# Attention scores on TensorE: seven bf16 parts in quarter columns, or two float32r parts in half rows

## The chip, the cores and the metric

One core of one Trainium2 chip runs the whole program in one launch. The metric is device time in microseconds, lower is better: the median of three runs of the kernel before is 895.65 us (894.32 to 899.57). The core has five engines that run side by side and wait for one another by semaphores: TensorE (PE in the profile; its weight loads are listed apart, as PEld), VectorE (DVE), ScalarE (ACT), GpSimd (POOL) and SyncE (SP, which here only issues DMA transfers).

## The reference, cut to what matters

The input is x of shape (2, 2048, 256) in float32. It is layer-normed to xn. Then the output is x plus a causal attention of xn plus a spectral feed-forward part of xn (a 256x256 matrix that the kernel works out once).

```
q = rope((xn @ wq).reshape(B, S, 16, 16)); k = rope((xn @ wk).reshape(B, S, 4, 16)); v = ... 4 heads
scores = einsum('bshd,bthd->bhst', q, k) / 4          # head_dim 16, 16 query heads on 4 key heads
attn   = softmax(where(causal, scores, -inf))
out    = x + einsum('bhst,bthd->bshd', attn, v).reshape(B, S, 256) @ wo + real(ifft(fft(xn) @ w)) + bias
```

The contraction of a score runs over only 16 dimensions, and it has to come out with nearly float32 exactness.

## The kernel before, in words

The 2 x 2048 rows are cut into 8 blocks of 512 rows: j = 0 to 3 along the sequence, b = 0 and 1 alternating. A block has four groups g of four query heads, so there are 32 units (n, g), eight for each j. Each unit works through its scores twice.

**First pass, row maxima (kind "A" in the planner).** `maxima` works out, for 128 rows and up to 512 keys, the scores with rows on the 128 partitions, and VectorE takes the maximum over the keys. Off the diagonal this is `row_max`: one PSUM tile `sm` holds two heads side by side (2 x 512 columns, two banks) and one TENSOR_REDUCE of 1024 elements reads it. On the diagonal, `first_rows` and `last_rows` build tiles `sd` whose 32-row pieces are laid out with turned order, so that masked parts are mostly left out: two tiles of 576 and four of 800 elements for a unit, reduced into `top_g`. `parts` puts the pieces together with two more reductions, splits the negated maxima into three bf16 parts with five further reductions, and `spread` turns them on TensorE (`ps_m`), copies them to `mt`, and sends `mt` by a DMA on ACT's queue into three rows of the unit's query tile `qst`.

**Second pass, probabilities (kind "B").** `scores` works out the same scores with keys on the partitions and 512 query rows as columns, the row maximum already subtracted by the three extra contraction rows (`kst` holds -1 there); ScalarE takes exp from PSUM (`st`, one bank for one head; `sp`, two banks, once all maxima are done) into `es`. For j > 0 GpSimd zeroes the masked triangles in `es`; for j = 0 TensorE adds a mask product. **Third, values (kind "V").** `values` multiplies `es` in float32 with `va` into `av` (four heads in four 32-column strips of TensorE), ScalarE copies `av` to `avs`, and a chain of DMAs, a reciprocal and a multiplication on GpSimd makes `attT`, from which `output` works out `po`, to which VectorE adds the residual `xr`.

**How a float32 score is made.** Rotated q and k (`raw`) are split on GpSimd (on VectorE for the first block) into three bf16 parts h, m, l by `split`: cast, subtract, cast, subtract. Seven products of parts are stacked along the contraction: `QPART = "hmlhmhm"` against `KPART = "hhhmmll"`, 7 x 16 = 112 rows, plus three for the maximum = 115 rows. The stacks `qst` and `kst` are filled by DMAs from SP (`stack`, `stack_runs`, the latter through a copy in HBM). Every product of the kernel except the transposes runs through `matmul` with 32 output partitions, four such instructions side by side in four column strips (`product`), which makes 128 partitions.

**What sets the order.** The kernel writes its own order, one instruction list per engine. A planner loop at the end keeps a clock for each engine, gives each piece a cost and the pieces it needs, and at each step picks among A, B, V, S (`spread`), F (late pieces) and M (other pieces). `due`, `AHEAD`, `RATE` and `WINDOW` say how far the maxima run ahead. The costs only shape the order; on the chip each engine takes its list in order and waits on semaphores. PSUM has eight banks: three of `st`, two double banks of `s` (`sm`, `sd`, later `sp`) and one of `av`.

Of the kernel before, what the change touches and what calls it, by code (L numbers as in the profile page):

```python
# [11 lines left out]
BF16 = mybir.dt.bfloat16  # L12
AF = mybir.ActivationFunctionType
# [4 lines left out]
P = 128  # L18
# [5 lines left out]
def tile_attn_plus_spectral_ffn(  # L24
# [47 lines left out]
    QPART = "hmlhmhm"  # L72
    KPART = "hhhmmll"
    KC = DH * len(QPART)
    KA = KC + 3
# [43 lines left out]
    def matmul(to, lhsT, rhs, **more):  # L119
        issued[0] += 2 if lhsT.dtype == BF16 else 4  # L120
        nc.tensor.matmul(to, lhsT, rhs, **more)  # L121
# [4 lines left out]

    def use(eng, us, needs=(), gives=()):
        clock[eng] = max(clock[eng], ready(needs)) + us
        if eng == "pe":
            at = issued[0] // LOADED  # L130
            for k in range(max(loaded), at + 1):
                clock["pe"] = max(clock["pe"], loaded[k])
                loaded[k + 1] = clock["pe"] + LOAD
            clock["pe"] = max(clock["pe"], loaded[at])
        for k in gives:
            there[k] = clock[eng] + LATE[eng]

# [47 lines left out]
    def load_x(n):  # L185
# [25 lines left out]
    ident_h = const.tile([P, P], BF16, name="ident_h")  # L211
    nc.vector.tensor_copy(ident_h, ident)

    mask = const.tile([P, P], BF16, name="mask")
    nc.gpsimd.memset(mask, 0.0)
    nc.gpsimd.affine_select(
        out=mask, in_=mask, pattern=[[-1, P]], compare_op=ALU.is_ge, fill=NEG, base=0,
        channel_multiplier=1,
    )

    mask_t = const.tile([P, P], BF16, name="mask_t")
    nc.gpsimd.memset(mask_t, 0.0)
    nc.gpsimd.affine_select(
        out=mask_t, in_=mask_t, pattern=[[1, P]], compare_op=ALU.is_ge, fill=NEG, base=0,
        channel_multiplier=-1,
    )
# [8 lines left out]

    turned_h = const.tile([P, P], BF16, name="turned_h")
    for q in range(0, P, QD):
        nc.vector.tensor_copy(turned_h[:, q : q + QD], ident_h[:, P - QD - q : P - q])

    G0, TE, TO, STEP = 10, 7, 35, 19
    top_g = const.tile([P, 2, NKV, 3 * STEP], F32, name="top_g")
    nc.vector.memset(top_g, NEG)
    nc.vector.memset(top_g[:, :, :, 0:3], 0.0)
    nc.vector.memset(top_g[:, :, :, 38:41], 0.0)
    rows_g = top_g.rearrange("p r h c -> p (r h) c")
    nc.gpsimd.affine_select(
        out=rows_g[:, :, 0:3], in_=rows_g[:, :, 0:3], pattern=[[0, 2 * NKV], [-QD, 3]],
        compare_op=ALU.is_ge, fill=NEG, base=-QD, channel_multiplier=1,  # L250
    )
    nc.gpsimd.affine_select(
        out=rows_g[:, :, 38:41], in_=rows_g[:, :, 38:41], pattern=[[0, 2 * NKV], [QD, 3]],
        compare_op=ALU.is_ge, fill=NEG, base=QD - 1, channel_multiplier=-1,
    )
# [157 lines left out]

    xnT, va, kst, qst = {}, {}, {}, {}

    def ones(n):
        e, eng, us = nc.gpsimd, "pool", 2.5 if n == 0 else 2.9
        va[n] = const.tile([P, NI, NKV, QD], F32, tag=f"va{n}", name=f"va{n}")
        e.memset(va[n], 1.0)
        kst[n] = const.tile([P, NKV, SB], BF16, tag=f"kst{n}", name=f"kst{n}")  # L420
        for h in range(NKV):
            e.memset(kst[n][96:P, h, :], -1.0)
        use(eng, us, (), [("ones", n)])

    def project(n):
# [99 lines left out]
        def stack(c, a_part, f):  # L525
            src = part[c][f * HP : (f + 1) * HP, "hml".index(a_part), :]
            for a in range(len(QPART)):
                if (KPART if c == NK else QPART)[a] == a_part:
                    to = kst[n] if c == NK else qst[n, 2 * c + f]
                    gives = []  # L530
                    if a == len(QPART) - 1 if c == NK else a_part == "l":
                        gives = [("kst", n) if c == NK else ("stk", n, 2 * c + f)]
                        gives += [("part", at[c, "part"])] * (c == NK)
                    needs = [("part", "in", n, c, a_part)]
                    later(to[a * DH : (a + 1) * DH, :, :], src, 64, needs, gives)

        def stack_runs(c, units):

            runs = {}
            for f in units:  # L540
                g = 2 * c + f
                runs[g] = dram.tile([3, HP, SB], BF16, tag="run", bufs=4, name=f"run{n}_{g}")
                later(
                    runs[g].rearrange("a r s -> r a s"), part[c][f * HP : (f + 1) * HP, :, :],
                    192, [("part", "in", n, c, "l")],
                    [("run", n, g)] + [("part", at[c, "part"])] * (f == 1),
                )
            for g, run in runs.items():
                rows = run.rearrange("a (d h) s -> (a d) (h s)", h=NKV)
                for lo, hi in ((0, 3), (3, 5), (5, 7)):  # L550
                    later(
                        qst[n, g][lo * DH : hi * DH, :, :], rows[0 : (hi - lo) * DH, :],
                        64 * (hi - lo), [("run", n, g)], [("stk", n, g)] * (hi == 7),
                    )
# [18 lines left out]
        def split(c, k):  # L573
            r = rows(c)
            if k == 0:
                if c < NK:
                    for g in (2 * c, 2 * c + 1):
                        qst[n, g] = work.tile(
                            [P, NKV, SB], BF16, tag="qst", bufs=8, name=f"qst{n}_{g}"
                        )  # L580
                        take_slot("qst")
                part[c] = work.tile([P, 3, SB], BF16, tag="part", bufs=3, name=f"part{n}_{c}")
# [5 lines left out]
            elif k == 1:  # L588
                ra[c] = work.tile([P, SB], F32, tag=f"ra{min(n, 1)}", bufs=1, name=f"rb{n}_{c}")
                e.tensor_tensor(ra[c][:r], raw[c][:r], part[c][:r, 0, :], ALU.subtract)  # L590
                use(eng, SUB, (), [("raw", at[c])])
            elif k == 2:
                e.tensor_copy(part[c][:r, 1, :], ra[c][:r])
                use(eng, CAST, (), [("part", "in", n, c, "m")])
                if direct(c, 0):
                    stack(c, "m", 0)
            else:
                e.tensor_tensor(part[c][:r, 2, :], ra[c][:r], part[c][:r, 1, :], ALU.subtract)
                use(eng, SUB, (), [("part", "in", n, c, "l")])
# [21 lines left out]
        for c in (NK, 0, 1):  # L621
# [6 lines left out]
                (eng, [], [], lambda c=c: split(c, 2)),  # L628
                (eng, [], [], lambda c=c: split(c, 3)),
# [6 lines left out]
    np_of, np_parts, made = [], [], []  # L636
    for a in range(2):
        of = const.tile([P, NI, 3, NKV, 2], F32, name=f"np_of{a}")
        nc.vector.memset(of, 0.0)
        np_of.append(of)  # L640
        np_parts.append(
            of.rearrange("p i a h b -> p (i a h b)").bitcast(BF16)
            .rearrange("p (i a h b) -> p i a h b", i=NI, a=3, h=NKV)[:, :, :, :, 3]
        )

    def maxima(n, g):
        b, j = blocks[n]
        t = {}
        slots, slots_done = [], []

        def begin():
            if not slots_done:
                t["mx"] = work.tile(
                    [P, 2, 2, NKV, NJ], F32, tag="mx", bufs=3, name=f"mx{n}_{g}"
                )
            slots_done.append(1)

        def pair_of(name):
            t["slot"] = take_slot("s")
            t["ps"] = ps_s.tile([P, 2, SB], F32, tag="s", name=name)  # L660

        def rows_of(h, i, q):

            at = i * P + (q if i % 2 == 0 else P - QD - q)
            return qst[n, g][0:KC, h, at : at + QD]

        def on_pe(k, us):
            use(
                "pe", us,
                [("stk", n, g), ("kst", at_block[b, k]), ("s", t["slot"] - ring["s"])],  # L670
                [("pair", t["slot"])],
            )

        def on_dve(cols, out, of):
            nc.vector.tensor_reduce(out, of, AX.X, ALU.max)  # L675
            use("dve", 0.07 + cols / 960, [("pair", t["slot"])], [("s", t["slot"])])

        def row_max(i, k, pr):


            def head(e):
                if e == 0:
                    begin()
                    pair_of(f"sm{n}_{g}_{i}_{k}_{pr}")
                h = 2 * pr + e
                on_pe(k, SB * 4.28e-4 + 0.003)
                for q in range(0, P, QD):
                    matmul(
                        t["ps"][q : q + QD, e, :], rows_of(h, i, q),
                        kst[at_block[b, k]][0:KC, h, :], start=True, stop=True,  # L690
                    )
                if e == 1:
                    r, odd = divmod(i, 2)
                    on_dve(2 * SB, t["mx"][:, odd, r, 2 * pr : 2 * pr + 2, k], t["ps"])

            needs = [("stk", n, g), ("kst", at_block[b, k])]
            return lambda: head(0), lambda: head(1), 2 * SB + 150, needs

# [3 lines left out]
        def keys(h, lo, hi):  # L702
            return kst[n][0:KC, h, lo:hi]

# [805 lines left out]
```

## Time and profile before

| what | value |
|---|---|
| median of three runs | 895.65 us (894.32 to 899.57) |
| the profiled execution, first to last instruction (its span; the profile gives no other time for it) | 892.9 us |
| what lies around the span, against the median | 2.75 us |
| granted TensorE clock | 1.000 |
| groups of scores for the maxima: `sm` matmuls, `sd` tiles | 3072 matmuls, 192 tiles |
| ScalarE exponentials | 1006 of one bank, 41 of two |
| transfers | 62.67 MB, mean 70 GB/s |

The page gives each engine's busy time over the span, and a chain of work that is followed back from the last instruction. A matmul's duration in the profile includes the time to fill and drain the array; matmuls of a stream overlap, so what one costs is read from the distance between starts, or from the chain, and not from its duration. A number of matmuls such as "x8" next to a time means eight 32-column instructions, that is two heads of 128 partitions.

### The profile page before, as it was taken

How to read it: one execution, taken by the hardware profiler on the slowest of the kernel's cores; microseconds unless marked ns; L12 is line 12 of the kernel's file. 1: busy time of each engine (PE TensorE's matmuls, PEld its weight loads, DVE VectorE, ACT ScalarE, POOL GpSimd, SP SyncE). 2: the span in 40 equal slices, each digit the busy share in tenths (PEclk: the TensorE clock that was granted, in tenths of full speed). 3: DMA queues.
4: the chain of work that ended last, by engine and by line, in shares of the span. 5: the costliest groups of instructions: out<-in, count | busy, mean ns of one | idle time of the engine just before them, and what ended most of it. 6: DMA issues, size and time to landing. Idle time of an engine off the chain costs nothing.

```text
span 892.9 us, 37137 instructions
## 1 busy us (share of the span) xinstructions
PE 877.8 (98%) x16596; PEld 475.6 (53%) x16596; DVE 728.6 (82%) x1002; ACT 637.1 (71%) x1188; POOL 364.1 (41%) x491
## 2 busy tenths in 40 slices
PE   8999999999999999999999999999999999999997
PEld 5666555555555555555544555565455555545443
DVE  7888887897969995999978899979889889798401
ACT  4276737687768875888747877858597887579885
POOL 8778757725933334631357121212652011101111
PEclk9999999999999999999999999999999999999999
DMA  5555733521451002430014300110241001100000
GB/s 180 133 148 135 203 96 96 160 71 39 111 148 62 27 29 83 106 106 14 20 50 120 97 28 14 39 51 14 60 115 60 14 3 40 50 14 15 27 2 25
DMA packets 42543, 62.67 MB, mean 70 GB/s; under 512 B 9080, under 2 KB 32360, under 8 KB 42384
## 3 DMA queue, kind: packets, MB, share of 16 engines
q1 hardware_dynamic: 32960, 41.83, 17.4%
q0 software_dynamic: 8128, 17.69, 6.2%
q8 instruction: 130, 2.13, 1.1%
q10 hardware_dynamic: 1296, 0.79, 0.3%
q14 instruction: 29, 0.24, 0.1%
HBM read 32.75 MB, written 18.40 MB: 57 GB/s over the span
## 4 chain that ended last, share of the span: by engine, by line
PE 90%; DVE 4%; ACT 3%; DMA 1%; issue 1%; ACTq 0%; SPq 0%; POOL 0%; DVEq 0%; POOLq 0%
PE av L121 25%; PE st L121 24%; PE sm L121 19%; PE sd L121 7%; PE po L121 6%; PE ps_q L121 4%; ACT es L946 2%; PE sp L121 2%; DVE top_g L675 2%; PE idle L125 1%; PE ps_x L125 1%; DMA qst<-run 1%; PE ps_ff L121 1%; PE ps_m L121 1%; DVE mx L675 1%
## 5 line engine op out<-in xcount | busy, mean ns | idle before, releaser
L946 ACT ACTIVATE es<-st 128x512 f32<-128x512 f32 x1006 | 533.1, 604 | 153.7 <-PE st L121 133.3
L675 DVE TENSOR_REDUCE mx<-sm 128x2 f32<-128x1024 f32 x384 | 450.0, 1216 | 39.2 <-PE sm L121 38.2
L121 PE MATMUL st<-qst,kst 115*32 115x512 bf16 (+9 forms) x4744 | 337.1, 345 | 0.2
L121 PE MATMUL av<-es,va 128*32 128x512 f32 (+3 forms) x2560 | 288.9, 529 | 1.3 <-ACT avs L1017 0.4
L121 PE MATMUL sm<-kst,qst 112*32 112x512 bf16 x3072 | 236.2, 379 | 0.7 <-DMA qst<-run 0.4
L121 PEld LDWEIGHTS <-kst 115*32 115x32 bf16 x5120 | 162.3, 95 | 136.0 <-issue 58.4
L121 PEld LDWEIGHTS <-qst 112*32 112x32 bf16 x5632 | 150.3, 96 | 128.0 <-issue 83.0
L675 DVE TENSOR_REDUCE top_g<-sd 128x25 f32<-128x800 f32 (+1 forms) x192 | 168.2, 906 | 35.3 <-PE sd L121 34.5
L964 POOL TENSOR_SCALAR_AFFINE_SELECT es<-es 128x512 f32<-128x512 f32 (+1 forms) x120 | 65.3, 546 | 236.1 <-ACT es L946 234.7
L121 PEld LDWEIGHTS av<-es,va 128*32 128x32 f32 x2560 | 82.2, 109 | 48.3 <-issue 18.3
L121 PE MATMUL sd<-kst,qst 112*32 112x384 bf16 (+11 forms) x2560 | 101.3, 256 | 2.3 <-DVE top_g L675 1.8
L1038 POOL DMA_DIRECT2D res<-avs x30 | 18.0, 601 | 105.7 <-ACT avs L1017 102.6
L121 PEld LDWEIGHTS <-ident_h 128*32 128x32 bf16 x1344 | 45.5, 96 | 27.0 <-issue 20.1
L1152 DVE TENSOR_TENSOR xr<-po,xr 128x256 f32<-128x256 f32 x36 | 15.2, 423 | 48.7 <-PE po L121 45.7
L121 PE MATMUL sd<-mask,ident_h 128*32 128x64 bf16 x1024 | 52.9, 193 | 0.1
L121 PE MATMUL ps_q<-xnT,wp 128*32 128x512 f32 x384 | 46.7, 594 | 0.2 <-ACT xnT L460 0.2
L946 ACT ACTIVATE es<-sp 128x1024 f32<-128x1024 f32 x41 | 39.7, 1027 | 6.1 <-PE sp L121 5.9
L475 ACT COPY raw<-ps_q 128x512 f32<-128x512 f32 x24 | 14.1, 587 | 34.9 <-PE ps_q L121 30.2
L560 POOL TENSOR_TENSOR ra<-raw,cs 128x512 f32<-128x512 f32 (+1 forms) x21 | 27.1, 1290 | 23.6 <-ACT raw L475 22.7
L121 PE MATMUL po<-wo_sb,attT 128*32 128x256 f32 x512 | 34.2, 380 | 0.0
L121 PE MATMUL po<-mff,xnT 128*32 128x256 f32 x512 | 33.7, 379 | 0.0
L1063 POOL DMA_DIRECT2D sums<-den x15 | 8.1, 540 | 61.7 <-DVE den L1057 61.7
(112 smaller groups left out, 614.2 us busy)
## 6 DMA issues: line engine op xcount, KB each, us to landing
qst<-run SPq DMA_DIRECT2D x62, 128.0 KB
res<-avs POOLq DMA_DIRECT2D x30, 256.0 KB, 2.9
run<-part SPq DMA_DIRECT2D x31, 192.0 KB
qst<-run SPq DMA_DIRECT2D x31, 192.0 KB
sw<-raw SPq DMA_DIRECT2D x70, 64.0 KB
xr<-in_L_attn_x_dram SPq DMA_DIRECT2D x16, 256.0 KB
attT<-res POOLq DMA_DIRECT2D x15, 256.0 KB, 4.2
inv<-sums POOLq DMA_DIRECT2D x15, 256.0 KB, 3.6
```

Of the source, the lines that this page charges most:

```text
L121: nc.tensor.matmul(to, lhsT, rhs, **more)
L125: nc.tensor.transpose(to, of, unit)
L475: nc.scalar.copy(raw[c], ps)
L560: e.tensor_tensor(ra[c][:r], raw[c][:r], cs[j][:r, 0, :], ALU.mult)
L675: nc.vector.tensor_reduce(out, of, AX.X, ALU.max)
L946: nc.scalar.activation(to, of, AF.Exp, scale=SCALE)
L964: nc.gpsimd.affine_select(out=to, in_=to, pattern=pattern, compare_op=ALU.is_ge, fill=0.0, base=0, channel_multiplier=-1,)
L1038: nc.gpsimd.dma_start(out=res[n, c][f], in_=avs[u])
L1063: nc.gpsimd.dma_start(out=sums, in_=den[n, c])
L1152: nc.vector.tensor_tensor(xr[n, r][:, e, :], po, xr[n, r][:, e, :], ALU.add)
```

## The change

* `split` makes two parts: h is `raw` rounded to float32r (a 4-byte type of TensorE), l is what is left, rounded. `QPART, KPART = "hlhl", "hhll"`: four products of 16 rows, the last cut by two dimensions, 62 rows, plus two for the maximum = 64 rows. Two of four GpSimd steps of `split` go.
* Heads of even number stand in rows 0 to 63 of `qst` and `kst`, heads of odd number in rows 64 to 127; a tile holds two heads along the columns. One score product is one instruction of 64 rows with 128 output partitions, and the one for the other half (the other head, another PSUM bank) follows it (`side_by_side`). Values, projections and outputs stay in 32-column strips.
* Diagonal row scores: five whole tiles of 1024 elements for a unit (`second_rows`, two of `first_rows`, two of `last_rows`). Masks are added by bf16 products with `eye` and `over` (`shut`), two for each half. The layout tricks with `top_g`, `turned_h` go.
* `parts` is one reduction, one copy and one subtraction (in place of seven reductions). `spread` is one product with a 32x128 result, `mt` has two parts, and its two small DMAs for a unit are issued by SP (stream `lasts`), not by ACT.
* `stack` and `stack_runs` issue more and larger DMAs: a query tile is filled by four of 128 KB in the planner's count, `run` holds two 4-byte parts.
* The planner keeps a clock for each half of the rows, books a cost for the change between halves and 32-column strips, starts the later blocks' preparation eight tiles earlier (`- 8`), and has new rules for the pick: it prefers to stay with A and B once it works in halves. In the order that comes out, TensorE changes between kinds of tiling 697 times.

The diff, cut to its core:

```
-    QPART = "hmlhmhm"
-    KPART = "hhhmmll"
-    KC = DH * len(QPART)
-    KA = KC + 3
+    KC = HP - 2
+    QPART, KPART = "hlhl", "hhll"
...
+    def use_half(half, us, needs, gives):
+        at = max(pe_start(half), ready(needs))
+        if not halves[0]:
+            half_free[:] = [at, at]
+        halves[0] = True
+        clock["pe"] = at
...
-        kst[n] = const.tile([P, NKV, SB], BF16, tag=f"kst{n}", name=f"kst{n}")
+        kst[n] = const.tile([P, 2, SB], F32R, tag=f"kst{n}", name=f"kst{n}")
...
+                for lane in range(2):
+                    for lo, hi in ((0, QD), (QD, KC)):
+                        later(
+                            qst[n, g][lane * HP + lo : lane * HP + hi].bitcast(F32),
+                            rows[lane, 0 : hi - lo],
+                            128, [("run", n, g)], [("stk", n, g)] * (hi == KC and lane == 1),
+                        )
...
-            elif k == 2:
-                e.tensor_copy(part[c][:r, 1, :], ra[c][:r])
...
+                e.tensor_tensor(
+                    part[c][:r, 1, :], raw[c][:r], part[c][:r, 0, :].bitcast(F32), ALU.subtract
+                )
...
+        for a in range(2):
+            dst, tri = to[:, starts[0] : starts[0] + P], over[kind][rows, a, :]
...
+            yield lambda dst=dst, tri=tri, a=a: add(dst, eye[rows, a, :], tri, a == 0)
...
+        def rows_of(h, i):
+            return qst[n, g][h % 2 * HP : h % 2 * HP + KC, h // 2, i * P : (i + 1) * P]
...
+            def lanes(to, lane):
+                h = 2 * pr + lane
+                yield lambda: add(to, rows_of(h, i), keys_of(h, k), True)
...
+            hl = work.tile([P, 2, 2, 2 * NI], F32R, tag="hl", bufs=2, name=f"hl{n}_{g}")
+            nc.vector.tensor_copy(high, mx)
+            nc.vector.tensor_tensor(low, mx, high.bitcast(F32), ALU.subtract)
...
-            nc.scalar.dma_start(out=qst[n, g][KC:KA, :, :], in_=mt)
+                nc.sync.dma_start(
+                    out=qst[n, g][at : at + 2].rearrange("a r s -> a (r s)").bitcast(F32),
+                    in_=mt[lane * DH : (lane + 1) * DH, :].bitcast(F32),
                 )
...
         for tile_t, row, at in parts:
+            add(
+                ps[:, at : at + SB - row], kb[heads, pr, tile_t * P : (tile_t + 1) * P],
+                rows[:, row:], not masked,
+            )
...
-        at = next(k for k, d in enumerate(due) if d >= a_from[NG * n])
+        at = next(k for k, d in enumerate(due) if d >= a_from[NG * n]) - 8
```

## The prediction

> **What bounds the kernel now.** I read the page's busy times first, then the chain that ended last, then the costliest groups, then two short stretches in which single streams can be timed.
>
> ```profile
> PE 877.8 (98%) x16596; PEld 475.6 (53%) x16596; DVE 728.6 (82%) x1002; ACT 637.1 (71%) x1188; POOL 364.1 (41%) x491
> ...
> PE 90%; DVE 4%; ACT 3%; DMA 1%; issue 1%; ACTq 0%; SPq 0%; POOL 0%; DVEq 0%; POOLq 0%
> PE av L121 25%; PE st L121 24%; PE sm L121 19%; PE sd L121 7%; PE po L121 6%; PE ps_q L121 4%; ACT es L946 2%; PE sp L121 2%; DVE top_g L675 2%; PE idle L125 1%; PE ps_x L125 1%; DMA qst<-run 1%; PE ps_ff L121 1%; PE ps_m L121 1%; DVE mx L675 1%
> ```
>
> PE never rests, and the chain is PE's own queue. Of the 892.9 us span, the scores that the change remakes hold `st` + `sp` 26% (232 us), `sm` 19% (170) and `sd` 7% (62.5): 464 us. But DVE (728.6) stands close behind, and any gain has to fit over it.
>
> ```profile
> L946 ACT ACTIVATE es<-st 128x512 f32<-128x512 f32 x1006 | 533.1, 604 | 153.7 <-PE st L121 133.3
> L675 DVE TENSOR_REDUCE mx<-sm 128x2 f32<-128x1024 f32 x384 | 450.0, 1216 | 39.2 <-PE sm L121 38.2
> ...
> L675 DVE TENSOR_REDUCE top_g<-sd 128x25 f32<-128x800 f32 (+1 forms) x192 | 168.2, 906 | 35.3 <-PE sd L121 34.5
> ```
>
> A whole reduction occupies DVE 450.0/384 = 1.172 us, one exp ACT 533.1/1006 = 0.530 us. The chain in the middle of the run gives the stream rates:
>
> ```profile
> 501.10 0.43 PE st L121 x8
> 501.53 0.43 PE sm L121 x8
> 501.96 0.50 PE st L121 x8
> 502.47 0.86 PE av L121 x8
> ```
>
> Two heads take 0.43 us, so 512 bf16 columns cost 0.217 us for one head; float32 `av` takes 0.86 for 512 columns of four heads. The `st` ahead of `av` costs 0.07 more. The timeline of PE shows what it costs to leave the 32-column strips for the full array and to return:
>
> ```profile
> 212.80 0.62 PE L121 MATMUL sm<-kst,qst 112*32 112x512 bf16 x8
> 213.35 1.09 PE L125 MATMUL ps_x<-ident,xt 128*128 128x128 f32 x8
> 214.37 0.61 PE L121 MATMUL sm<-kst,qst 112*32 112x512 bf16 x8
> ```
>
> The first `sm` stream ends at 212.80 + 2 x 0.217 = 213.23, the transposes start at 213.35: 0.12 us. The last of them starts at 213.35 + 1.09 - 0.27 (its own duration, from the tile's view) = 214.17 and streams 128 columns (0.05); the next `sm` starts at 214.37: 0.15 us. A change of tiling costs 0.13 us on average.
>
> **The change part by part.** No row of this profile shows a float32r product, two row halves at work, or a product with 64 rows and 128 output columns. The largest term rests on that.
>
> *Streams.* I price a float32r column like a bf16 one. The bounds are bf16 (0.217 for 512 columns) and float32 (0.86). I take the first, because the profile shows each float32 product as two load-and-matmul records (`av`: 2560 records for 1277 instructions of the order), passes over parts of the value, and a value that is rounded already needs one. Two halves together then do two heads in 0.217.
> - `sm`: 384 pairs x 0.217 = 83 us, was 170.
> - `st`, `sp`: a unit has 2 x ((4j+2) x 512 + 256) pair columns, 278,528 over 32 units, x 0.217/512 = 118, and j = 0 masks 16,384 columns = 7: 125 us, was 232.
> - `sd`: a unit has 5 x 512 score columns and 2048 mask columns, 147,456 in all = 62.5 us, was 62.5. Whole tiles give back what the halves win.
>
> Together 270 for 464: -194 us.
>
> *Halves out of step.* PE starts matmuls in the order in which they stand, as all starts in this trace do, so a head on half 0 followed by a pair makes half 1 wait. Walking the order in which the changed kernel's instructions stand, each instruction starting no sooner than its predecessor and when its half is free, gives 309 us where perfect pairs give 257 (masks included, `sp` apart): +52. Bounds 0 (every head finds a partner) to +232 (halves in turns).
>
> *Changes of tiling.* 697 in the new order, 53 in the old: 644 x 0.13 = +84 us. Bounds 0.10 to 0.20 us each: +64 to +129. The 0.07 ahead of `av` (276 places, 19 us) may fall into this; I count half, -10.
>
> *Weight loads.* A load of 128 columns is new. The eight transposes follow each other at about 0.109 us ((1.09 - 0.27)/7.5), set by such loads. Loads here hide behind streams: two heads on the same 112 rows in 0.43. I take 0, which is also the low end, since no load is exposed in these streams now. The high end is that the 3360 loads queue one behind another at 0.109: the same walk gives 438 instead of 309, +129.
>
> The Trainium skill speaks against this ("TensorE: Matmul & The Clock Gate", Part 3, The mechanism): a weight load overlaps a running matmul only where the row group differs. By that rule each half would show its own load, and the walk would give some 200 us more, an estimate with the page's rule. The row just named contradicts it for column strips; for halves nothing here shows it.
>
> *DVE.* Reductions of tiles: 544 x 1.172 = 637.5, was 618.2: +19. `parts`: seven small reductions, 53 us by their groups, become three at about 0.27, 0.19 and 0.19: 21 us, -32. Block 0 loses a cast and a subtraction for each part: -4. DVE ends at 712 us, and doesn't shrink with PE.
>
> *ACT, POOL, SP.* `mt` goes from 0.57 us to that of a 128x128 copy, 0.27, x 32 = -10 on ACT. POOL loses 14 x (0.61 + 1.17) + 7 x 1.76 = 37 us. Both lie beside PE and give nothing; if that cover goes, they are gains. SP issues about 100 more DMAs, off the path while DMA is 20% busy. The two `mt` transfers of a unit now stand in SP's queue, behind whatever waits there: SP sat 304.6 us in all before output transfers that waited for `xr`. In the new order five units' `mt` follow such a transfer directly; `st` of the next unit and all behind it on PE would wait. The planner's lead of three to five steps covers it; uncovered at 5 us each +25. I take 0.
>
> *What is late next.* Take a j = 3 unit. PE: (5.2 `sm` + 2.0 `sd` + 6.3 `st`) x 1.2 for halves + 12.5 `av` + 2.8 `po` and `ps_q` + 34 changes x 0.13 = 36. DVE: 29 x 1.172 + 0.65 + 0.42 = 35. ACT: 58 x 0.530 + 1.5 = 32. Three engines stand within 10%, and two double banks couple them. Summing, unit by unit, the longer of PE and DVE gives 19 us over PE alone. I take +25 for new waits, bounds 0 to +65.
>
> *Sum.* 892.9 - 194 + 52 + 84 - 10 + 25 = 850 us span; the median stands 2.75 above its span: 852 us.
>
> **The rivals.**
> *DVE floor, faster.* If halves stay in step and changes cost 0.10: 852 - 26 - 19 - 25 waits = 782; but DVE needs 712 plus some 50 at the end (from 840 on it is nearly idle) and 20 to 30 of thin start, about 790. For it: DVE's idle time is now mostly waits for PE. Against: the order already shows heads without partner.
> *Loads not hidden, slower than before.* If 128-column loads queue on one path, +129: 981 us. It decides from the point where the 309 us of half-row work grow by 43, 14%: 0.217 for a pair becoming 0.25. For it: loads are four times as wide as now, and transposes are bound by them. Against: 0.43 us for two heads with every load hidden.
> *Halves take turns.* +232: about 1084. Half rate for float32r (the walk at double column cost, +300) 1150, float32 rate 1700 and more. Then the change doesn't do what it says. For it: nothing shown excludes it. Against: only that separate column strips do run together here.
> *No difference.* Changes of tiling at 0.20 give +45: 897.
>
> **How the numbers follow.** Main case 0.64, its own range 807 (changes at 0.10, half the lane loss) to 890 (waits at +65). DVE floor 0.08. Loads partly or wholly exposed 0.13 (890 to 985). Turns or load exposed in each half 0.09. Slower float32r 0.06. The range 805 to 985 leaves out the last two and the floor's lower part, about 0.19. A measurement of this kernel tells 0.5% from no change, 891.2 to 900.1. Faster: 0.08 + 0.62 of the main case = 0.70. The same: 0.02 of the main case and 0.02 of the exposed loads = 0.04. Slower: 0.11 + 0.09 + 0.06 = 0.26.
>
> **What would show it.** Right: `sm` pairs 0.22 us apart with both halves starting together; about 0.13 us at each change of tiling; DVE busy near 712 and over 80%; PE busy falling to about 800; `st` + `sm` on the chain under 30%. Wrong: starts of one half 0.3 us or more apart for 512 columns (loads), the second half starting when the first ends (turns), 0.2 us and more at each change, or PE idle at a new unit with `mt` as releaser.

## The result, and the profile after

| | before | after |
|---|---|---|
| median on the same chip, 20 runs each | 895.25 us (893.82 to 899.57) | 898.28 us (895.25 to 901.75) |
| ratio | | 1.0031, 95% interval 1.0019 to 1.0042 |
| profiled execution, span | 892.9 us | 893.5 us |
| PE busy | 877.8 us | 866.4 us |
| DVE, ACT busy | 728.6, 637.1 us | 723.9, 621.2 us |

The change makes no difference that counts: 3 us slower, where 44 us faster were forecast (852 for 895.65); the time lies inside the stated range, 46 us above its main figure. One execution of all those below, the profiled one of the first run with bf16 operands, took 1521 us for a reason that isn't known, and its profile is not read. The page of the changed kernel, busy times and the chain that ended last:

```profile
PE 866.4 (97%) x7796; PEld 404.8 (45%) x7796; DVE 723.9 (81%) x832; ACT 621.2 (70%) x1188; POOL 330.5 (37%) x434
...
PE 85%; DVE 6%; ACT 3%; DMA 2%; issue 2%; POOL 1%; SPq 1%; ACTq 0%; POOLq 0%
PE av L120 28%; PE st L120 22%; PE sm L120 11%; PE sd L120 8%; PE po L120 6%; DVE top L710 5%; PE ps_q L120 5%; ACT es L901 3%; PE sp L120 1%; PE ps_m L120 1%; PE ps_x L124 1%; PE ps_ff L120 1%; DMA sums<-den 1%; SPq L457 1%; DMA xt<-in_L_attn_x_dram 0%
```

PE issues less than half as many products and is still busy for 97% of the span. `sm` fell from 19% of the chain to 11%, as forecast; `st`, which lost half its columns too, only from 24% to 22%; VectorE and ScalarE, together 7% before, hold 9%. So the end is still PE's own queue, and the halved streams gave their time to something on PE. The groups (busy, mean ns of one, then the idle time of the engine just before them and what ended it), with weight loads among them:

```profile
L901 ACT ACTIVATE es<-st 128x512 f32<-128x512 f32 x1006 | 527.6, 601 | 196.1 <-PE st L120 194.6 <-PE sd L120 0.4
L710 DVE TENSOR_REDUCE top<-sm 128x2 f32<-128x1024 f32 x384 | 452.4, 1218 | 48.6 <-PE sm L120 47.8
L120 PEld LDWEIGHTS st<-qst,kst 64*128 64x128 f32 x1186 | 150.4, 185 | 192.3 <-ACT es L901 154.1 <-issue 10.0 <-ACT raw L493 8.8
L120 PEld LDWEIGHTS sm<-kst,qst 62*128 62x128 f32 x768 | 85.8, 185 | 52.9 <-DVE top L710 32.1 <-issue 11.2 <-PE ps_m L120 3.4
L120 PEld LDWEIGHTS <-eye 64*128 64x128 bf16 x800 | 31.7, 95 | 44.1 <-issue 34.5
```

A float32r weight load takes 185 ns, a bf16 one of the same 64 rows and 128 columns 95. ScalarE still waits for `st` (194.6 us, 133.3 before), although two heads now come side by side in the time of one. One stretch of PE's timeline, matmuls first, then the loads of the same stretch (start, length of the group, shapes, count; in brackets the idle time ahead of it):

```profile
540.55 1.06 PE L120 MATMUL av<-es,va 128*32 128x512 f32 x8
541.55 0.49 PE L120 MATMUL st<-qst,kst 64*128 64x512 f32 x2
...
544.63 0.90 PE L120 MATMUL sm<-kst,qst 62*128 62x512 f32 x4
545.37 0.63 PE L120 MATMUL st<-qst,kst 64*128 64x512 f32 x3
545.93 1.07 PE L120 MATMUL av<-es,va 128*32 128x512 f32 x8
```

```profile
541.55 0.19 PEld L120 LDWEIGHTS st<-qst,kst 64*128 64x128 f32 x2 [0.84 <-ACT es L901]
...
545.03 0.19 PEld L120 LDWEIGHTS sm<-kst,qst 62*128 62x128 f32 x2 [0.21 <-DVE top L710]
545.14 0.42 PEld L120 LDWEIGHTS st<-qst,kst 64*128 64x128 f32 x3
```

The `st` pair at 541.55 comes out of the strips: its load starts with it, and each product of the pair has a record of 0.49 us. Where a load starts behind a running stream (545.14, behind the `sm` pair that started at 545.03), the `st` products that follow at 545.37 have records of 0.39 us. The difference, 0.105 us, is a load that stands open: nothing streams in its half meanwhile. 522 of the 826 `st` records of 512 columns are long in this way (median 0.492 us, shortest 0.385), and 313 of the 768 of `sm`.

**An account of PE.** The records can be laid one behind another, each from its start to its end less 0.165 us. A column is counted at 0.417 ns (the shortest records are 0.212 us for 128 columns and 0.372 for 512, in the variant with bf16 operands below), and 0.165 is what the median bf16 record of 512 columns of the kernel before, 0.379 us, has over its columns. With the 0.159 of the shortest records instead, some 7 us of the changed kernel move from gaps into streams of scores. Sums over the profiled executions, us:

| where PE's time goes | before | after | difference |
|---|---|---|---|
| streams of scores and masks | 481.0 | 389.3 | -91.7 |
| of these after: columns of perfect pairs | | 266.2 | |
| of these after: heads without partner | | 46.7 | |
| of these after: open float32r loads, the rest | | 76.4 | |
| gaps between streams, within strips | 25.0 | 2.9 | -22.1 |
| gaps between streams, within halves | 0 | 30.0 | +30.0 |
| gaps at changes of tiling (53 and 696) | 7.1 | 76.0 | +68.9 |
| `av`, `po`, `ps_q` | 333.3 | 348.0 | +14.7 |
| all else | 42.4 | 43.3 | +0.9 |
| sum | 888.8 | 889.5 | +0.7 |

The sum agrees with the difference of the spans, 0.6 us. With bf16 operands the same rule gives 315 us of streams of scores and masks, 75 us less. By place, counted only where nothing else streams in the load's own half, the open loads come to some 70 us: entry into halves from the strips 34, behind a wait within halves 15, behind a mask product 8, behind other streams 13.

### The profile page after: what moved, and what is told of

It is laid out like the page before. It is cut to its first block, busy times and chain, and to the rows that moved or that the text cites. A ratio compares the mean times of both kernels' runs of the same rounds, so it can differ in the third digit from the quotient of the medians.

```text
span 893.5 us, 19337 instructions
## 1 busy us (share of the span) xinstructions
PE 866.4 (97%) x7796; PEld 404.8 (45%) x7796; DVE 723.9 (81%) x832; ACT 621.2 (70%) x1188; POOL 330.5 (37%) x434
## 4 chain that ended last, share of the span: by engine, by line
PE 85%; DVE 6%; ACT 3%; DMA 2%; issue 2%; POOL 1%; SPq 1%; ACTq 0%; POOLq 0%
PE av L120 28%; PE st L120 22%; PE sm L120 11%; PE sd L120 8%; PE po L120 6%; DVE top L710 5%; PE ps_q L120 5%; ACT es L901 3%; PE sp L120 1%; PE ps_m L120 1%; PE ps_x L124 1%; PE ps_ff L120 1%; DMA sums<-den 1%; SPq L457 1%; DMA xt<-in_L_attn_x_dram 0%
## 5 line engine op out<-in xcount | busy, mean ns | idle before, releaser
L901 ACT ACTIVATE es<-st 128x512 f32<-128x512 f32 x1006 | 527.6, 601 | 196.1 <-PE st L120 194.6
L710 DVE TENSOR_REDUCE top<-sm 128x2 f32<-128x1024 f32 x384 | 452.4, 1218 | 48.6 <-PE sm L120 47.8
L120 PE MATMUL st<-qst,kst 64*128 64x512 f32 (+3 forms) x1186 | 308.3, 413 | 1.4 <-ACT es L901 0.6
L120 PEld LDWEIGHTS st<-qst,kst 64*128 64x128 f32 x1186 | 150.4, 185 | 192.3 <-ACT es L901 154.1
L710 DVE TENSOR_REDUCE top<-sd 128x2 f32<-128x1024 f32 (+2 forms) x160 | 191.1, 1218 | 43.0 <-PE sd L120 42.4
L120 PE MATMUL sm<-kst,qst 62*128 62x512 f32 x768 | 177.2, 431 | 3.1 <-DVE top L710 2.8
L120 PEld LDWEIGHTS sm<-kst,qst 62*128 62x128 f32 x768 | 85.8, 185 | 52.9 <-DVE top L710 32.1
L120 PE MATMUL sd<-kst,qst 62*128 62x128 f32 (+3 forms) x512 | 89.2, 371 | 1.4 <-DMA qst<-part 1.4
L120 PE MATMUL sd<-over_rows,eye 64*128 64x256 bf16 (+1 forms) x640 | 65.3, 253 | 3.2 <-DVE top L710 3.2
L120 PEld LDWEIGHTS <-eye 64*128 64x128 bf16 x800 | 31.7, 95 | 44.1 <-issue 34.5
L120 PEld LDWEIGHTS sd<-kst,qst 62*128 62x128 f32 x512 | 49.8, 187 | 2.4 <-DMA qst<-part 1.5
L588 POOL TENSOR_TENSOR ra<-raw,cs 128x512 f32<-128x512 f32 (+1 forms) x21 | 26.8, 1278 | 46.7 <-ACT raw L493 43.5
```

The lines of the kernel that those rows point to most:

```text
L588: e.tensor_tensor(ra[c][:r], raw[c][:r], cs[j][:r, 0, :], ALU.mult)
L710: nc.vector.tensor_reduce(to, reads(ps), AX.X, ALU.max)
L901: nc.scalar.activation(to, of, AF.Exp, scale=SCALE)
```

## The experiments

Theory L: the weight load that comes with a float32r product stands open. Theory W: PE, VectorE and ScalarE wait for one another. Theory P: PE's own queue is full, above all with changes of tiling. Ratios are to the kernel before on the same chip; the changed kernel stands at 1.0031. Where one needs a time, "898" is that kernel's median.

**VectorE and ScalarE made light, alone and together, and the same on the kernel before (W).** The edits:

```
-                nc.vector.tensor_reduce(to, reads(ps), AX.X, ALU.max)
+                seen = reads(ps)[..., : w // 4]
+                nc.vector.tensor_reduce(to, seen, AX.X, ALU.max)
...
-            nc.scalar.activation(to, of, AF.Exp, scale=SCALE)
+            few = SB if es_slot[u, t, pr] < 2 * ES else SB // 4
+            nc.scalar.activation(to[..., :few], of[..., :few], AF.Exp, scale=SCALE)
```

> The changed kernel with the same order, but each reduction over a score tile reads only a quarter of its columns (the maxima are taken over a quarter of the keys), about 0.34 us for 1.17. Theory W (the time went into waits between PE, DVE and ACT, which now stand close together): DVE's busy time falls by some 450 us, PE no longer waits for its double banks, time falls by 20 to 40 us. Theory P (PE's own queue is full: changes of tiling, weight loads that stand open, halves without a partner): less than 8 us.

> The changed kernel with the same order, but from the 17th buffer on each exp of one bank writes only the first quarter of its columns (the rest of a probability tile is old data), about 0.22 us for 0.53. Theory W: PE waits for st banks less often, time falls by 20 to 40 us. Theory P: less than 8 us.

> Both of the two before it at once: maxima over a quarter of the keys, exps over a quarter of the columns. What is left is PE's own queue. Theory W: about 835 us, the sum of PE's streams, changes and entry loads without waits. Theory P: 880 us or more, PE busy 97% as before.

> The same two cuts in the kernel before (maxima over a quarter of the columns, exps over a quarter), as the control: both theories expect little, 875 to 893 us, since PE was busy 98% there and its chain held hardly a wait.

Measured: reductions alone 886.69 us, 0.9903 (0.9888 to 0.9918); exponentials alone 872.57, 0.9741 (0.9716 to 0.9767); both 848.69, 0.9461 (0.9429 to 0.9494); both on the kernel before 876.79, 0.9805 (0.9772 to 0.9837). Reductions alone fall between what W and P expected, exponentials alone are in W's range, both together are again between the two. So waits cost the changed kernel 51 us (0.0570 of 895) and the kernel before 18: 33 us are new. The page of the changed kernel with both light:

```profile
PE 829.6 (98%) x7796; PEld 394.0 (46%) x7796; DVE 318.0 (37%) x832; ACT 321.7 (38%) x1188; POOL 329.7 (39%) x434
```

PE is busy for 829.6 us, and 465 of the 826 `st` records still show an open load. By the account, gaps within halves fall from 30 to 15 us, and the streams of scores by 28, since heads wait less for a partner and fewer loads stand behind a wait. W is a part, not the whole.

**More changes of tiling (P).** A bf16 product of 32 columns by 32 is put ahead of 177 products, so that PE leaves the halves and returns:

```
+        if e == 1 and pr == 0 and d < 0 and wide[pr] is None:
+            nc.tensor.matmul(ps[0:QD, 0:QD], eye[:, 0, 0:QD], eye[:, 0, 0:QD], ...)
```

> The changed kernel with 177 tiny products of 32x32 in the 32-column tiling put in front of score products of the second half (their result is overwritten by the score product): 177 more round trips between halves and strips, nothing else. If a round trip costs what the trace of after shows at the values (0.10 in, 0.10 of open weight load, 0.11 out, 0.03 the product) and PE is the bound (theory P), +50 to +65 us. If PE has slack under ACT and DVE (theory W), +25 us or less.

Measured: 929.70 us, 1.0371 (1.0341 to 1.0402): 30 us, between what W and P expected. In the records, 25 of the 177 added products come directly behind values, where PE is in the strips already, so that 152 round trips are added and not 177: 0.20 us each. The parts in the records are about 0.10 out, 0.10 in and 0.105 of load. By the account the gaps at changes grow by 27 us and the streams of scores, with their open loads, by 10, and gaps within halves fall by 6: the changes show in full, the loads only in part. That some of them stood open already, or take the place of waits, is likely but not shown.

**The kind of product (L).** First a control, float32r operands that are always the same (`kst[0]`, with `exp` scaled down), then bf16 constants, whose loads are bf16 loads:

```
-        rows = qst[n, g][heads, pr, :]
+        rows = kst[0][heads, pr, :]                                  (the control; its maxima likewise)
...
+        part = eye[lane * HP : lane * HP + rows, 1 - lane, :]
...
-            add(ps[:, at : at + SB - row], kb[heads, pr, ...], rows[:, row:], not masked)
+            plain(ps[:, at : at + SB - row], e, HP, not masked)     (the bf16 constants)
```

> Control for the next: every score product takes its float32r operands from the first block's keys (so no score is right, and exp has a thousandth of the scale), with the same order and shapes; no product waits for query tiles. Both theories: like the changed kernel, within 8 us, if the waits for transfers were short.

> Every score product has its shape and place, but both operands are a small constant in bf16 (no score is right), so that its weight load is an instruction of its own, which carries no wait and can run ahead. Against the control before it: if the loads that come with a float32r product cost the time (theory L: 0.10 us at each of 322 entries into halves, and 0.1 us or more at each product that waits for a bank), 50 to 100 us less. If not, 0 to 15 us less.

> The score products with constant bf16 operands once more (their values leave out the scores, their shapes, order and waits stay), this time for the record of the execution: about 850 us, span about 847. If the weight load that comes with a float32r product is what was lost (L), hardly any st or sm stream of 512 columns shows the 0.105 us of an open load, where with float32r 522 of 826 and 313 of 768 did, and the pairs stand 0.23 us apart. If it is the data or the waits (W), the share of long streams stays and only the distances between streams shrink.

Measured: the control 897.04 us, 1.0014 (0.9997 to 1.0032), no different from the changed kernel. With bf16 operands 850.25 us, 0.9476 (0.9443 to 0.9509), and in the second run 848.47, 0.9466 (0.9438 to 0.9494): 47 and 49 us below the control, just short of the 50 to 100 that L expected and far from the 0 to 15 named for the case without it. The second run's timeline, matmuls and loads at an entry, and its groups:

```profile
543.75 1.06 PE L120 MATMUL av<-es,va 128*32 128x512 f32 x8
544.74 0.39 PE L120 MATMUL st<-eye 64*128 64x512 bf16 x2
544.97 0.38 PE L120 MATMUL sm<-eye 62*128 62x512 bf16 x2
```

```profile
544.74 0.33 PEld L120 LDWEIGHTS <-eye 64*128 64x128 bf16 x6 [0.84 <-issue]
```

```profile
L120 PE MATMUL st<-eye 64*128 64x512 bf16 x826 | 212.3, 380 | 1.4 <-ACT es L904 0.7
L120 PEld LDWEIGHTS <-eye 64*128 64x128 bf16 x2080 | 112.0, 94 | 257.2 <-issue 224.7
```

The entry at 544.74 has the load and the pair starting together, as at 541.55 of the changed kernel, yet the products take 0.39 us and not 0.49. No `st` record of the 826 is long, 4 of `sm` are; adjacent pairs stand 0.226 us apart at the median (0.336 with float32r, 0.23 where its load was hidden). The open loads of the account are gone (streams of scores 75 us less). 51 us of that show in the time (0.0565 of 895); gaps within halves rise from 30 to 51 us, and the chain now has VectorE on it for 23% (6% with float32r):

```profile
PE 64%; DVE 23%; ACT 5%; issue 3%; POOL 3%; SPq 1%; DMA 1%; POOLq 0%; ACTq 0%; DVEq 0%
```

**Loads and waits together.** The bf16 operands and the light engines in one kernel:

> The bf16 operands and, beside them, reductions and exponentials over a quarter of their columns (both leave out the scores). Alone the first brought 47 us (L) and the second 49 (W). If open loads and waits are two losses, both come off: about 802 us. If a wait costs mainly because it opens the load that stands behind it, the two overlap: 825 to 845. If PE's own queue with its changes of tiling is the floor (P), no less than about 800 either way.

Measured: 790.92 us, 0.8834 (0.8801 to 0.8868), 107 us below the changed kernel: the 51 of the loads and the 51 of the waits add up, and 5 more; that is below the 802 expected of two losses, and below the 800 that was named as P's floor. They are two losses. What is left is PE's own queue:

```profile
PE 766.6 (97%) x7796; PEld 279.8 (35%) x7796; DVE 321.0 (41%) x832; ACT 318.7 (40%) x1188; POOL 327.9 (42%) x434
```

**The loads at the entry alone.** The first float32r product of each half after the strips is made the bf16 one, the other 1980 stay:

```
+        if lane in fresh:
+            fresh.discard(lane)
+            if lhsT.dtype == F32R:
+                plain(to, lane, lhsT.shape[0], first)
+                return
```

> Only the float32r product that comes first in each half after the strips (580 of 2560) takes constant bf16 operands, the rest stays as in the changed kernel; this leaves a part of the scores out, and exp scales by a thousandth of its factor. By the durations of the changed kernel's records these loads stood open for 32 us. L: that much comes off, or 20 us at the share (47 of 76 us) that the bf16 operands brought when all products had them: 866 to 878 us. W: the time goes into waits and the result is within 4 us of 898.

Measured: 872.37 us, 0.9744 (0.9726 to 0.9762): 26 us, in the middle of what L expected. Not quite a quarter of the products carries half of the loss of L.

**The masks.** The mask products on the diagonal maxima are left out:

```
-                yield from shut(to, lane, "rows", (3 * P,))
```

> The changed kernel without the mask products in the maxima's diagonal tiles (the maxima there run over later keys too). That takes 2048 columns of pair streams for each unit from PE, 65,536 in all, 28 us, and nothing from any other engine. Theory P: 25 to 35 us less. Theory W: less than 12 us.

Measured: 887.52 us, 0.9907 (0.9870 to 0.9944): 11 us for 28 us of streams, which is in W's range. By the account the streams of scores and masks fall by only 19 us, and gaps within halves grow by 10. Why the streams keep 8 us was not followed up in full; a part is loads that the masks had covered. A float32r product behind a mask of 256 columns (0.107 us) streams 0.01 to 0.02 us after it, so that most of the load is hidden there; behind a mask of 128 columns (0.053 us) it streams 0.07 to 0.08 us after it (`sd` of 512 columns: 0.475 us, 0.377 with bf16 operands).

**Other orders of the same work.** Values two steps at a time, and returning to scores less readily; then that order with light engines; returning more readily, with values as they were; two steps alone. A second step is taken only where it is soon ready, by the planner's clock within 2 us in the first order and 0.3 us in the last. The edits of the first, cut:

```
-    NEAR, FEW, STAY, FULL, SPARE = 0.2, 0.6, 0.5, 1.0, 0.5
+    NEAR, FEW, STAY, FULL, SPARE = 0.2, 0.1, 0.5, 1.0, 0.5     (values by twos; the eager order has 1.0 there and nothing else)
...
-        if "V" in soon and (lag > 1 or "M" not in soon):
+        if "V" in soon and (lag > 2 or "M" not in soon):
...
-            values(*steps[v_next])
-            v_next += 1
+            for _ in range(2):
+                values(*steps[v_next])
+                v_next += 1
...
+                if max(ready(values_need(*steps[v_next])), 0) > clock["pe"] + 2:
+                    break
```

> The same computation as the changed kernel, another order: the planner takes two steps of the values at a time and is less ready to leave the strips, so that there are 72 round trips between halves and strips fewer, and by the walk of the order 12 us less of halves without partner. P (own queue): at the 0.18 us of the added round trips -13 us, at the 0.35 us of their parts -25, with the better pairing up to -37: 861 to 885 us. W (waits): longer stretches of values starve VectorE and ScalarE, which stand within 10 percent of PE, and eat the gain: 890 to 905.

> The order with values by twos, which took 977 us, with reductions and exponentials over a quarter of their columns (this leaves most of the maxima and probabilities out). W: the 79 us were VectorE and ScalarE left without work and PE waiting for them later, so with light engines they go, and the 72 round trips that this order saves show at last: 849 us of the changed order with light engines, less 13 to 25, so 824 to 836. If the order stalls for another reason (GpSimd's masks, the es buffers, transfers), 860 to 900.

> The same computation as the changed kernel; the planner leaves the strips for scores already when VectorE or ScalarE has less than 1.0 us of work left in its book, not 0.6: 18 round trips more, by the walk of the order 4 us less of halves without partner. W: fed engines gain 5 to 15 us: 883 to 893. P: 18 x 0.18 to 0.35 less 4, so 897 to 900.

> The same computation as the changed kernel; two steps of the values at a time where the second is ready, but the strips are left as readily as in the changed kernel: 25 round trips fewer, by the walk 7 us less of halves without partner. P: -5 to -16: 882 to 893. W: a stretch of 1.7 us of values is longer than what ScalarE has in its three banks, so 10 to 30 us slower: 908 to 928.

Measured, against 898: 72 round trips fewer 977.17 us, 1.0892 (1.0841 to 1.0942); 25 fewer 929.34, 1.0385 (1.0367 to 1.0403); 18 more 984.16, 1.0993 (1.0974 to 1.1012); 72 fewer with light engines 862.41, 0.9631 (0.9609 to 0.9653), against 848.69 with light engines in the changed order. The first and the third lie far outside what was expected, on the slow side, the second just past the slow edge of W (928), the fourth in the range given for an order that stalls for another reason. The order with the fewest changes, its busy times and its waits:

```profile
PE 913.8 (93%) x7796; PEld 428.6 (44%) x7796; DVE 737.8 (75%) x832; ACT 618.7 (63%) x1188; POOL 329.1 (34%) x434
```

```profile
ACT es L901 <- PE st L120: 258.7, 241, 5.8
```

By the account it saves what was counted (gaps at changes to and from strips 59 for 69 us, entry loads 26 for 34) and loses more: gaps within halves 74.4 for 30.0, loads behind waits 22 for 15, gaps within strips 16.5 for 2.9. ScalarE waits 64 us longer for `st`. A part is the clock: the granted clock is 0.982 in this run, with 38 us of the span at 0.50 against 7 in the changed kernel, which is at most some 15 us. With light engines 65 of the 79 us are gone, so most of it goes back to waits, by the clock or directly (the clock stands at 0.50 for 7 us there too); but the order is even then 14 us slower than the changed one, and its 72 round trips never show as a gain. Why it stalls then is not settled: the values wait in it 13.3 us within strips, with nothing tried on that. The eager order failed in another way, told under the hardware below. No variant that does all the work was faster than either kernel.

## Why the prediction was wrong

The forecast was 852 us. With bf16 loads and the same order and shapes, the changed kernel takes 848. The step that failed is the term "weight loads: 0": 76 us of float32r loads stand open, and 51 us of the time go with them. That 848 comes so close to 852 is luck in part: in that run the streams, the heads without partner, the changes and the gaps within strips are together 48 us better than booked, the waits and the values 45 us worse.

- **Streams, -194: right in rate, short in what they replaced.** A float32r column costs what a bf16 column costs, to some 4%, and two halves run together: where the load is hidden, pairs stand 0.23 us apart (0.226 with bf16), both products starting within 0.01 us. The pairs' columns make 266 us (270 forecast). The rivals of a slower float32r and of halves in turns fall with that. The old streams held 481 us of the account, not the 464 of the chain: 17 us more gain than booked.
- **Halves out of step, +52:** 46.7 by the records, 47 with bf16 operands.
- **Changes of tiling, +84:** the gaps are 0.114 us out of halves and 0.099 in, below the 0.13 booked, and make +68.9. But each entry brings the open load, 34 us (a part of the 76 of the next term), and the first `av` behind a change a further 8. Together +111.
- **Weight loads, 0: the failed term.** 76 us stand open, 51 of them in the time. The price of a load was taken from the transposes (0.109 us apart) and its hiding from bf16 strips. Both rows were of other types: this load takes 0.185 us. Behind a stream of 256 columns or more (from 0.107 us) the next product of the half streams 0.01 to 0.03 us later, behind 128 columns (0.053 us) about 0.07 later, and where no stream runs 0.105 us stand open: at each of some 320 entries, and behind waits. The rival "loads not hidden" had the right mechanism with the wrong place: no queue of loads over all products (two halves load side by side, 4 ns apart), but one open load after each interruption. Its point of decision, 43 us more of half-row work, was passed.
- **Ahead of `av`, -10:** -22.1, the gaps within strips are nearly all gone.
- **New waits, +25:** 51 against 18, so +33, inside its bounds.
- **Values and projections, not booked:** `av`, `po` and `ps_q` hold 15 us more; 8 are the first `av` behind a change, the rest was not followed up.
- **DVE 712, ACT -10, POOL -37:** 723.9, -15.9 and -33.6; all beside PE. (The rival "DVE floor" takes off 26 for halves in step, which is half of the 52 that they would free; in full it would be 756 and not 782, below its own floor either way.) No unit waited for `mt` in a way that shows: PE's waits name ScalarE and VectorE, and the transfers have 0.4 us of `st`.

Of the signs of being wrong, starts 0.3 us apart for 512 columns came true (0.336 at the median of adjacent pairs). Of the signs of being right, both halves start together and DVE stands at 81%, but PE stayed at 866 us and not near 800, and `st` with `sm` at 33% of the chain, not under 30%. The rival "no difference" gave 897 with changes at 0.20 us: its number came close, since a change with its load costs 0.17 us by the account (111 + 7 of before, over 696), though not for the reason it gave, and other terms were off beside it. (An added round trip has two changes, so its 0.20 us is 0.10 a change: there the loads showed only in part.)

The Trainium skill's rule that spoke against the change ("TensorE: Matmul & The Clock Gate", Part 3, The mechanism: a load overlaps a running matmul only where the row group differs) is not what happened: the `st` loads at 545.14 run while `sm` streams in both halves, so in their own too. The same section also says that a load into the background weight buffer is pulled ahead of a running matmul, and that agrees. What would have helped is that page's Part 2, LDWEIGHTS, read with the section on weight-path modes: it prices a load by its columns alone, an estimate of 107 ns for 128, and says that the fast load of 128 columns is for types other than FP32. The runs have 94 ns for bf16 and 185 for float32r with the same 64 rows and 128 columns, so the type counts by a factor of two; the measurement decides over the formula.

Not settled: within halves, whether a load behind a wait is open because it is long or because the product's wait stands on it, since the bf16 variant changes both. At the entries it is the length: there the bf16 load runs no further ahead than the float32r one (both start some 0.095 us behind the end of the strips' stream, 4 and 2 ns ahead of their product), and yet the products take 0.386 us with bf16 and 0.497 with float32r.

## What to carry to other kernels

Price a product by its stream and its weight load in the type that it will have, and count the places where no stream runs ahead of it, which are changes of tiling, waits and very short products; with a load of 0.185 us, each of those costs up to 0.1 us that a rate per column doesn't show. Halving the work of the engine that carries the end pays only down to its neighbours: with DVE at 81%, ACT at 70%, and three single and two double banks of PSUM between them and PE, 51 us went to waits. Where an order stands in that balance, moving one knob of it in either direction can cost several times what the counted savings are worth.

## What the runs showed of the hardware that was not expected

**The clock falls without any long idle time.** In the eager order, maxima are bunched, and VectorE works without a break while PE feeds it a pair for each reduction. PE's granted clock over 40 slices, a table over short stretches (us, busy time and count of PE, PEld, DVE, ACT, POOL, then the granted clock, DMA share, GB/s), and PE's timeline:

```profile
PEclk9989999999997699999999995799999896999999
```

```profile
323.00:326.00 3.00, 1.44 (x12) 0.80 (x11) 3.00 (x4) 0.00 (x0) 0.52 (x2) 1.00 0.24 90
326.00:329.00 3.00, 1.54 (x6) 0.62 (x5) 3.00 (x4) 0.00 (x0) 0.71 (x2) 0.72 0.28 84
329.00:332.00 3.00, 2.46 (x14) 1.34 (x13) 3.00 (x4) 0.00 (x0) 0.00 (x0) 0.50 0.02 10
...
341.00:344.00 3.00, 3.00 (x18) 0.96 (x13) 2.08 (x6) 0.57 (x2) 1.16 (x2) 0.50 0.02 5
```

```profile
325.74 0.50 PE L120 MATMUL sm<-kst,qst 62*128 62x512 f32 x2 [0.63 <-DVE top L710]
326.87 0.51 PE L120 MATMUL sm<-kst,qst 62*128 62x512 f32 x2 [0.63 <-DVE top L710]
328.00 0.79 PE L120 MATMUL sm<-kst,qst 62*128 62x512 f32 x2 [0.62 <-DVE top L710]
```

PE was busy for half the time from 323 to 329, with no gap over 0.98 us, and the clock went to 0.50; the same pair then takes 0.79 us for 0.50. It stayed there until about 344, some 6 us after PE was fully busy again. Over the run the granted clock is 0.950, against 0.997 for the changed kernel, so part of the 86 us is the clock and part the bunched maxima; they were not separated. The Trainium skill ("TensorE: Matmul & The Clock Gate", Part 1, What's actually happening) describes a gate that follows how busy PE has been, halves the clock after an idle window of about 3.4 us and frees it after a busy one of the same length. The half clock agrees. Here it fell with no gap over 0.98 us, so an idle stretch of 3.4 us is not needed: some 3.4 us with PE half busy were enough. In the changed kernel it fell once in the middle of the run, at 131.0 us for 3.4 us, behind 3.4 us in which PE was busy for half the time with no gap over 0.63 us.

**A float32r load of 64 rows and 128 columns takes 0.185 us, a bf16 one 0.094, and a float32 load of 128 rows and columns 0.140**, and two halves load at the same time (4 ns apart). **A float32r product of rounded values streams at nearly bf16's rate**, pairs of 512 columns 0.23 us apart for 0.226.
